# Two chunks of channels multiplied for 15 steps of the q, k, v stage while the third chunk's statistics are made, and put back into PSUM in their steps

## The chip, the cores and the metric

The kernel runs on one core of a Trainium2 chip. A core has five engines, each with its own queue of instructions that it works off in order: TensorE (PE, with its weight loads shown apart as PEld), VectorE (DVE), ScalarE (ACT), GpSimd (POOL) and SyncE (SP, which here only issues transfers). ACT and POOL issue transfers as well. Matrix products land in PSUM[...]; everything else on the chip lies in SBUF. The metric is the device time of one execution in microseconds (us), lower is better. A change of less than 0.2% can't be told from none.

## The reference

The input x is one image of 384 channels and 192 x 192 pixels in fp32. Two layers follow each other, and both add to x. Only the first one's beginning matters here:

```
g  = group_norm(x, 32 groups of 12 channels, eps 1e-5)     # no gain, no offset
qkv = w_qkv (1152 x 384) @ g + b_qkv                       # at every pixel
qkv = max over 2 x 2 pixels                                # 96 x 96 left
qkv = depthwise 3 x 3 convolution + b_dw                   # 'SAME'
q, k, v = thirds of the channels; 8 heads of 48 channels
attn = (q/|q|) (k/|k|)^T over pixels, 48 x 48 per head; four top-k softmaxes, summed; times v
x = x + repeat2x2(gelu(...)) @ w_proj + b_proj
```

The second layer is again a group norm, followed by seven depthwise convolutions (up to 13 x 13) that the kernel has folded into one, and is added to x.

The group norm needs the mean and the variance of 12 channels over all pixels before the first product can be made, so x is read once for the statistics and again for the products.

## The kernel before, in words

The 384 channels are three chunks (`NJ`) of 128 partitions. A group has 12 channels, so chunks 0 and 1 together hold 21 whole groups and 4 channels of a 22nd, whose other 8 channels are the first of chunk 2.

**Statistics stage.** The first two row blocks of x, in halves, are loaded by SP as four tiles `xt` (`load`), all three chunks at once; they stay for the next stage. The rest of each chunk comes as 22 blocks (`NX`) of 1536 pixels, chunk after chunk, in tiles `xs` of a ring of ten, loaded by ACT's queue and SP's (`load_block`, L200). VectorE takes each in three `bn_stats` of 512 columns (L236), and after a chunk's last block one `bn_aggr` (L240) gives mean and variance per channel, `mv0`. `group_stats` then goes from channels to groups and back with tiny products (with the matrices `gm` and `gmt`): mean per group (L106), broadcast (L114), variance (L123), reciprocal square root (`rsqrt`, with one ACT step), broadcast of scale and offset (L134). It is a generator, so that its pieces can be put between other work; here it runs in one go (`in_one`). The result is `gn0`, scale and offset per channel (L244).

POOL meanwhile folds the seven filters into one, `wf`; SP writes it to memory (`wfd`) at the end of the stage.

**q, k, v stage.** A loop over 48 row blocks B: for B below 24 (`NB`) q and k are made, for the 24 after that v, with x read a second time. A block is 8 rows of pixels, worked in two halves `sb`; a step is one half and one chunk m of 128 output channels, so a q, k block has 12 steps and a v block 6. In a step:

- `project` makes 2 rows x 3 input chunks j of products with 384 columns (L350) into a PSUM tile `qkv`[...]. Two such tiles take turns. The trace counts two passes for each fp32 product.
- `pool`: VectorE takes the maximum of 2 x 2 pixels (L361), after which the step after next can use the PSUM tile, and ACT adds the bias and writes it into `pooled` (L368).
- `normalize` applies `gn0` to a third of a half of the next block's x on ACT (L327), in steps 6 to 11 of a block.
- after the second half of an m: `begin` on ACT (L381), eight taps of the depthwise convolution on VectorE in the second and third step after (`taps`, L397), and `end` on ACT in the fourth: the squares with their sum (L411) and the copy of two halo rows (L416).
- after the last m of a block, in steps 3 to 6 of the next: transposes of q and k (L426), their copies on ACT (L428) and the Gram products (L438).
- in step 8 of a q, k block `strip`, an ACT copy (L457), and POOL's transfers: parts of the filter matrices. They use the memory of `v`, which is empty until block 24.

The order inside the stages is written out (`manual_schedule`): each engine takes its instructions as the program names them. What stands outside such a stretch (clearing `pooled`, L314; loading biases, L276 to L280) is put by the planner where it is ready, and where its memory is free.

After it come attention, the projection and the second layer's convolution, which the change leaves as they are but for the pool that one small tile (`gx`) comes from.

Of the kernel before, what the change touches and what calls it, by code (L numbers as in the profile page):

```python
# [7 lines left out]
F32 = mybir.dt.float32  # L8
AF = mybir.ActivationFunctionType
ALU = mybir.AluOpType  # L10
AX = mybir.AxisListType
PSUM = bass.MemoryType.PSUM
DRAM = bass.MemoryType.DRAM

P = 128
C = 384
NJ = C // P
H = W = 192
HW = H * W
HS = WS = 96  # L20
NG = 32
HEADS = 8
CH = C // HEADS
NPR = HEADS // 2
P2 = 2 * CH
KEEP = (CH // 2, CH * 2 // 3, CH * 3 // 4, CH * 4 // 5)
BRANCHES = ((5, 1), (7, 1), (5, 2), (3, 3), (3, 4), (3, 5))
K0 = 13
# [7 lines left out]
BR, BC = 8, 16  # L36
# [21 lines left out]
def tile_attn_then_large_kernel_conv(ctx: ExitStack, tc: tile.TileContext, a: dict, out: bass.AP):  # L58
    nc = tc.nc
    x = a["x"]  # L60
# [16 lines left out]
    gm = const.tile([P, NJ, NG], F32, name="gm")  # L77
    nc.sync.dma_start(out=gm, in_=a["gm"].rearrange("(j p) g -> p j g", p=P))
    gmt = const.tile([NG, C], F32, name="gmt")
    nc.sync.dma_start(out=gmt, in_=a["gmt"])  # L80
# [19 lines left out]
    def group_stats(pool, psum, mv, name, js=range(NJ)):  # L100


        own = slice(js[0], js[-1] + 1)
        ps = psum.tile([NG, 1], F32, tag="gs", name=f"{name}_ps")
        for j in js:
            nc.tensor.matmul(ps, lhsT=gm[:, j, :], rhs=mv[:, j, 0:1], start=(j == js[0]), stop=(j == js[-1]))  # L106
        mean = pool.tile([NG, 1], F32, name=f"{name}_mean")
        nc.vector.tensor_copy(mean, ps)
        yield
        yield  # L110

        pb = psum.tile([P, NJ, 1], F32, tag="gs", name=f"{name}_pb")
        for j in js:
            nc.tensor.matmul(pb[:, j], lhsT=gmt[:, j * P : (j + 1) * P], rhs=mean, start=True, stop=True)  # L114
        s = pool.tile([P, NJ, 1], F32, name=f"{name}_s")
        nc.vector.tensor_sub(s[:, own], mv[:, own, 0:1], pb[:, own])
        nc.vector.tensor_mul(s[:, own], s[:, own], s[:, own])
        nc.vector.tensor_add(s[:, own], s[:, own], mv[:, own, 1:2])
        yield
        yield  # L120
        pv = psum.tile([NG, 1], F32, tag="gs", name=f"{name}_pv")
        for j in js:
            nc.tensor.matmul(pv, lhsT=gm[:, j, :], rhs=s[:, j], start=(j == js[0]), stop=(j == js[-1]))  # L123
        var = pool.tile([NG, 1], F32, name=f"{name}_var")
        nc.vector.tensor_copy(var, pv)
        r = yield from rsqrt(pool, var, 1e-5, name)
        sb = pool.tile([NG, 2], F32, name=f"{name}_sb")
        nc.vector.tensor_copy(sb[:, 0:1], r)
        nc.vector.scalar_tensor_tensor(sb[:, 1:2], mean, -1.0, r, ALU.mult, ALU.mult)
        yield  # L130
        yield
        pc = psum.tile([P, NJ, 2], F32, tag="gs", name=f"{name}_pc")
        for j in js:
            nc.tensor.matmul(pc[:, j], lhsT=gmt[:, j * P : (j + 1) * P], rhs=sb, start=True, stop=True)  # L134
        return pc

    def in_one(gen):

        while True:
            try:  # L140
                next(gen)
            except StopIteration as e:
                return e.value


    R = 4
    NB = HS // R
# [16 lines left out]
    mv0 = const.tile([P, NJ, 2], F32, name="mv0")  # L164
    with (
        tc.tile_pool(name="s1", bufs=1) as s1,
        tc.tile_pool(name="sx", bufs=10) as sx,
# [7 lines left out]
        FX = 2 * R * 2 * W  # L175
        FB = 1536
        NX = (HW - FX) // FB
        NS0 = 2 * 2 * 2
        stats = s1.tile([P, NJ, NS0 + NX * (FB // 512), 6], F32, name="stats")
# [13 lines left out]
        xss = []  # L193

        def load_block(n):
            j, b = divmod(n, NX)
            xt = sx.tile([P, FB], F32, name=f"xs_{n}", tag="xs")

            eng = nc.scalar if n < 8 or n % 2 == 1 else nc.sync
            eng.dma_start(out=xt, in_=x[j * P : (j + 1) * P, FX + b * FB : FX + (b + 1) * FB])  # L200
            xss.append(xt)

        for n in range(2):
            load_block(n)
# [6 lines left out]
        for n in range(2, 10):  # L211
            load_block(n)
# [16 lines left out]

        for n in range(NJ * NX):  # L230
            if n in (1, 3, 5, 7):
                rows_stats(n // 2)
            j, b = divmod(n, NX)
            xt = xss.pop(0)
            for q in range(FB // 512):
                nc.vector.bn_stats(stats[:, j, NS0 + b * (FB // 512) + q, :], xt[:, q * 512 : (q + 1) * 512])  # L236
            if n + 10 < NJ * NX:
                load_block(n + 10)
            if b == NX - 1:
                nc.vector.bn_aggr(mv0[:, j, :], stats[:, j].rearrange("p n s -> p (n s)"))  # L240
        nc.sync.dma_start(
            out=wfd.rearrange("(j p) s -> p j s", p=P), in_=wf.rearrange("p j x y -> p j (x y)")
        )
        nc.vector.tensor_copy(gn0, in_one(group_stats(s1, s_ps, mv0, "g0")))  # L244
# [7 lines left out]
    with ExitStack() as ctx_v:  # L252
        vpool = ctx_v.enter_context(tc.tile_pool(name="vpool", bufs=1))
        NM = 3 * NJ
        NEG = -(2.0**127)
        v = vpool.tile([P, NJ, HS, WS], F32, name="v")
        ssq = vpool.tile([P, 2 * NJ, NB], F32, name="ssq")
        bd = vpool.tile([P, NPR, P], F32, name="bd")
        ctx_a, ctx_qk = ExitStack(), ExitStack()
        gps = ctx_a.enter_context(tc.tile_pool(name="gram", bufs=1, space=PSUM))  # L260
        gram = gps.tile([2 * CH, NPR, 2 * CH], F32, name="gram")
        a2 = ctx_a.enter_context(tc.tile_pool(name="a2", bufs=1))
        aw = ctx_a.enter_context(tc.tile_pool(name="aw", bufs=1))
        qkvps = ctx_a.enter_context(tc.tile_pool(name="qkvps", bufs=2, space=PSUM))
# [4 lines left out]
        wqk = a1.tile([P, NJ, 2 * C], F32, name="wqk")  # L269
        wv = a2.tile([P, NJ, C], F32, name="wv")  # L270
        wqkv = a["wqkvT"].rearrange("(j p) o -> p j o", p=P)
# [20 lines left out]

        free = v.rearrange("p j h w -> p (j h w)")
        ZQ = 32 * NJ // NB
# [30 lines left out]
        def normalize(B, sb, j):  # L325
            xt = xts[B, sb]
            nc.scalar.activation(xt[:, j], xt[:, j], AF.Identity, bias=gn0[:, j, 1:2], scale=gn0[:, j, 0:1])  # L327
# [14 lines left out]

        def project(B, m, sb):

            ps = qkvps.tile([P, SR, 512], F32, tag="qkv", name="qkv")
            xt = xts[B, sb]
            wq, mm = (wqk, m) if m < 2 * NJ else (wv, m - 2 * NJ)
            for r in range(SR):
                for j in range(NJ):
                    nc.tensor.matmul(  # L350
                        ps[:, r, : 2 * W],
                        lhsT=wq[:, j, mm * P : (mm + 1) * P],
                        rhs=xt[:, j, r * 2 * W : (r + 1) * 2 * W],
                        start=(j == 0),
                        stop=(j == NJ - 1),
                    )
            return ps
# [284 lines left out]
        def begin_attention():  # L642
# [4 lines left out]

        steps = [
            (B, u, (2 * NJ if B >= NB else 0) + u // 2, u % 2)
# [3 lines left out]
        with tc.manual_schedule():  # L653
            nc.sync.dma_start(out=wqk, in_=wqkv[:, :, : 2 * C])
# [4 lines left out]
            for s, (B, u, m, sb) in enumerate(steps):  # L659
# [8 lines left out]
                pool(m, sb, project(B, m, sb))  # L668
# [46 lines left out]
        with (  # L715
            tc.tile_pool(name="bx", bufs=3) as bx,
            tc.tile_pool(name="b1", bufs=1) as b1,
# [28 lines left out]
            with tc.manual_schedule():  # L746
# [13 lines left out]
                for b in range(NBB):  # L760
# [19 lines left out]
                    g = b1.tile([P2, NBK], F32, tag="gx", name=f"gx_{b}", bufs=3)  # L780
# [441 lines left out]
```

## Time and profile before

| what | us |
|---|---|
| median of three runs | 3096.77 (3096.74 to 3097.59) |
| the profiled execution | 3095.74 |
| its span | 3094.0 |
| statistics stage, to the last `bn_aggr` | 0 to 154.1 |
| group statistics | 154.1 to 160.7 |
| a block of q and k (12 steps), TensorE's time | 50.46 |
| TensorE busy over the span | 2913.6 (94%) |
| VectorE busy | 2529.4 (82%) |
| ACT busy | 1247.2 (40%) |
| POOL busy | 915.6 (30%) |

A row of the chain names what the end of the program was waiting for at that time, so time taken out elsewhere is worth nothing until the chain moves there. A row of the groups gives line, engine, operation, tile written and read, shapes and count, then busy time, mean length in ns, and the engine's idle time before it with what ended it. Lengths of neighbouring instructions overlap a little: 66 `bn_stats` of 676 ns each took 39.12 us, 593 ns from start to start. Such spacings, not lengths, add up to time.

### The profile page before, as it was taken

The numbers are of one execution on the slowest core, as the hardware profiler recorded it, in microseconds if no ns is written. First come the engines' busy times: TensorE is split into PE (matmuls) and PEld (weight loads), VectorE is DVE, ScalarE is ACT, GpSimd is POOL, SyncE is SP. The second block draws the span as 40 slices with busy tenths as digits, with TensorE's granted clock in tenths as the row PEclk, the third lists the DMA queues.
The fourth block names the chain that finished last, engine by engine and source line by source line (L and its number), as shares of the span: only waits on it lengthen the run. The fifth ranks groups of instructions, "written<-read, shape, count | busy, mean of one in ns | idle before, by whom it ended". The sixth has DMA issues, their size and how long they took to land.

```text
span 3094.0 us, 31922 instructions
## 1 busy us (share of the span) xinstructions
PE 2913.6 (94%) x10794; PEld 1938.3 (63%) x10794; DVE 2529.4 (82%) x3459; ACT 1247.2 (40%) x2339; POOL 915.6 (30%) x1103
## 2 busy tenths in 40 slices
PE   0099999999999999999999999999999999999998
PEld 0056666666666666666555555555777777777776
DVE  8968887878787878788999899878778777777775
ACT  0034444444444444444444444733333333333332
POOL 3033232424232323222223222500433333333331
PEclk9999999999999999999999999999999999999999
DMA  9933433334342424233333332577999999999994
GB/s 386 383 113 96 136 107 121 124 108 143 89 153 77 155 80 152 87 122 104 125 104 101 103 128 71 168 217 198 263 263 247 241 247 246 246 248 244 244 218 116
DMA packets 276307, 523.95 MB, mean 169 GB/s; under 512 B 26866, under 2 KB 190768, under 8 KB 276144
## 3 DMA queue, kind: packets, MB, share of 16 engines
q1 hardware_dynamic: 204880, 327.00, 39.6%
q0 software_dynamic: 45040, 151.32, 16.2%
q10 hardware_dynamic: 26224, 43.59, 3.8%
q8 instruction: 86, 1.41, 0.2%
q14 instruction: 77, 0.63, 0.1%
HBM read 360.46 MB, written 161.37 MB: 169 GB/s over the span
## 4 chain that ended last, share of the span: by engine, by line
PE 87%; DVE 10%; DMA 1%; issue 1%; ACT 0%; POOL 0%; SPq 0%; ACTq 0%; DVEq 0%; POOLq 0%
PE qkv L350 49%; PE conv L1012 29%; PE pj L1074 3%; DVE stats L236 3%; DVE v L397 3%; PE av L770 2%; PE gram L438 2%; PE tr L426 2%; DVE mx L361 1%; DMA xs<-in_x 1%; DMA xt<-in_x 1%; DVE xp L994 0%; DVE cell L1090 0%; DVE stats_t L1091 0%; DVE mv L240 0%
## 5 line engine op out<-in xcount | busy, mean ns | idle before, releaser
L350 PE MATMUL qkv<-xt,wqk 128*128 128x384 f32 x3456 | 1132.6, 487 | 1.3 <-ACT xt L327 1.3
L350 PEld LDWEIGHTS qkv<-xt,wqk 128*128 128x128 f32 x3456 | 650.3, 190 | 435.7 <-ACT xt L327 2.1
L1012 PE MATMUL conv<-xp,wt 128*128 128x288 f32 (+1 forms) x3840 | 917.7, 402 | 2.5 <-ACT co L1020 2.5
L1012 PEld LDWEIGHTS conv<-xp,wt 128*128 128x128 f32 x3840 | 729.0, 190 | 188.8 <-ACT co L1020 2.9
L397 DVE SCALAR_TENSOR_TENSOR acc<-pooled,wd,acc 128x384 f32<-128x384 f32 (+2 forms) x1152 | 732.8, 636 | 30.6
L361 DVE TENSOR_REDUCE mx<-qkv 128x192 f32<-128x768 f32 x432 | 412.6, 955 | 241.0 <-PE qkv L350 229.3
L368 ACT ACTIVATE pooled<-mx,bq 128x192 f32<-128x192 f32 x432 | 196.8, 456 | 962.1 <-DVE mx L361 961.8
L994 DVE STREAM_TRANSPOSE xp<-xn 128x4608 f32<-128x4608 f32 (+1 forms) x107 | 442.1, 4132 | 173.2 <-PE conv L1012 165.7
L350 PE MATMUL qkv<-xt,wv 128*128 128x384 f32 x1728 | 563.8, 487 | 1.7 <-ACT xt L327 1.1
L350 PEld LDWEIGHTS qkv<-xt,wv 128*128 128x128 f32 x1728 | 325.6, 190 | 234.4 <-ACT xt L327 7.5
L1020 ACT ACTIVATE co<-conv,cb 128x288 f32<-128x288 f32 x384 | 191.1, 499 | 598.0 <-PE conv L1012 587.8
L335 POOL TENSOR_TENSOR sum<-xt 128x192 f32<-128x192 f32 x144 | 97.2, 675 | 1109.8 <-ACT xt L327 1097.5
L397 DVE SCALAR_TENSOR_TENSOR v<-pooled,wd,v 128x384 f32<-128x384 f32 (+2 forms) x576 | 376.6, 654 | 15.2
L327 ACT ACTIVATE xt<-xt,gn 128x768 f32<-128x768 f32 x288 | 285.2, 1014 | 2.9 <-DVE gn L244 2.9
L1037 POOL DMA_DIRECT2D out<-o x191 | 105.8, 584 | 567.3 <-DVE o L1028 519.2
L971 POOL TENSOR_TENSOR raw<-raw,up 128x2496 f32<-128x2496 f32 x46 | 230.8, 5016 | 26.8 <-DMA up<-pd 26.8
L1028 DVE STREAM_TRANSPOSE o<-co 128x2304 f32<-128x2304 f32 (+1 forms) x50 | 209.9, 4201 | 19.8 <-ACT co L1020 19.8
L106 PE MATMUL g_ps<-mv,gm 128*32 128x1 f32 x18 | 1.8, 186 | 156.3 <-DVE mv L240 153.6
L1074 PE MATMUL pj<-v,wp 128*128 128x384 f32 x432 | 144.2, 493 | 0.6 <-ACT gx L781 0.6
L236 DVE BATCH_NORM_STATS2 stats<-xs 128x6 f32<-128x512 f32 x198 | 118.2, 676 | 1.8 <-DMA xs<-in_x 1.7
L1074 PEld LDWEIGHTS pj<-v,wp 128*128 128x128 f32 x432 | 81.9, 192 | 56.0 <-ACT gx L781 1.2
L336 POOL TENSOR_TENSOR sum<-sum,xt 128x192 f32<-128x192 f32 x144 | 113.2, 786 | 11.3
(171 smaller groups left out, 1730.7 us busy)
## 6 DMA issues: line engine op xcount, KB each, us to landing
xt<-in_x SPq DMA_DIRECT2D x96, 1152.0 KB, 7.2
wt<-zd SPq DMA_DIRECT2D x46, 1536.0 KB, 13.1
raw<-in_x SPq DMA_DIRECT2D x182, 312.0 KB, 13.1
out<-o POOLq DMA_DIRECT2D x188, 288.0 KB, 6.8
zd<-v POOLq DMA_DIRECT2D x96, 416.0 KB, 4.6
up<-pd SPq DMA_DIRECT2D x184, 156.0 KB, 12.2
xs<-in_x ACTq DMA_DIRECT2D x37, 768.0 KB, 13.1
xs<-in_x SPq DMA_DIRECT2D x29, 768.0 KB, 15.0
```

Of the source, the lines that this page charges most:

```text
L236: nc.vector.bn_stats(stats[:, j, NS0 + b * (FB // 512) + q, :], xt[:, q * 512 : (q + 1) * 512])
L327: nc.scalar.activation(xt[:, j], xt[:, j], AF.Identity, bias=gn0[:, j, 1:2], scale=gn0[:, j, 0:1])
L350: nc.tensor.matmul(ps[:, r, : 2 * W], lhsT=wq[:, j, mm * P : (mm + 1) * P], rhs=xt[:, j, r * 2 * W : (r + 1) * 2 * W], start=(j == 0), sto ...
L361: nc.vector.tensor_reduce(mx, ps[:, :, : 2 * W].rearrange("p r (y w x) -> p r w y x", y=2, x=2), AX.XY, ALU.max,)
L368: nc.scalar.activation(pool_t[m][:, k : k + SR, 1 : 1 + WS], mx, AF.Identity, bias=bq[:, m : m + 1])
L397: nc.vector.scalar_tensor_tensor(acc[:, :nt], pool_t[m][:, k0 + dy : k0 + dy + nt, dx : dx + WS], wd[:, m, t : t + 1], acc[:, :nt], ALU.mu ...
L971: eng.tensor_add(rv, rv, uv.unsqueeze(2).to_broadcast([P, (m1 - m0) * WS, 2]))
L994: nc.vector.transpose(bass.AP(at.tensor, at.offset, [list(at.ap[0]), [NBQ, n], [1, NBQ], [NQ * NBQ, CC], [ME * NBQ, NE]],), bass.AP(row.te ...
L1012: nc.tensor.matmul(ps[:, t0:t1], lhsT=wt[:, c, o : o + P], rhs=d[:, c, g + 2 * t0 : g + 2 * t1 - 1 : 2, :], start=(g == 1), stop=(g == NGR ...
L1020: nc.scalar.activation(co[:, c], ps, AF.Identity, bias=cb[:, cc : cc + 1])
L1028: nc.vector.transpose(bass.AP(at.tensor, at.offset, [list(at.ap[0]), [2 * W, n], [BC, NBQ], [W, 2], [1, BC]]), bass.AP(of.tensor, of.offse ...
L1074: nc.tensor.matmul(ps, lhsT=wp[:, j, i * P : (i + 1) * P], rhs=v[:, j, b * RB : (b + 1) * RB, :].rearrange("p r w -> p (r w)"), start=(j = ...
```

## The change

After chunk 1's statistics are done, and while those of chunk 2 are made, scale and offset of chunks 0 and 1 are worked out (the group that reaches into chunk 2 gets its eight missing channels from a transfer of their own, `spare`, with statistics `sy`). With them TensorE multiplies chunks 0 and 1 for the first half (`sb` 0) of row blocks 0 to 4 and the three q chunks: 15 steps, list `EARLY`. Each result is copied by ACT from PSUM to `begun`. In the step itself ACT copies it back into a PSUM tile (`fill`, one step ahead), and `project` only adds the products of chunk 2.

What this takes along:

- `v`, `wqk` and the PSUM tiles of the q, k, v stage are set up before the statistics stage. The x blocks that the early products read stay (`kept`, in the memory of `v`); so do the results. Of the ring of ten, five tiles lie in `v` as well.
- `group_stats` can have a further column (`NJ`, the eight channels), and with `apart` it yields between a product and its reader. `early` is advanced once after each `bn_stats` of chunk 2; after its small operations it names all its products in one piece. The final group statistics use chunks 1 and 2 only.
- of `wqk`, the q columns of chunks 0 and 1 are loaded late in chunk 0; the rest after the last x block. Odd blocks of chunk 2 are loaded by POOL's queue in place of ACT's.
- the steps of a q, k block go q0, k0, q1, k1, q2, k2 in place of q0, q1, q2, k0, k1, k2.

```diff
-    gm = const.tile([P, NJ, NG], F32, name="gm")
+    GY = 2 * P // (C // NG)
+    NY = (GY + 1) * (C // NG) - 2 * P
+    gm = const.tile([P, NJ + 1, NG], F32, name="gm")
...
+    gmt = const.tile([NG, C + P], F32, name="gmt")
+    nc.sync.dma_start(out=gmt[:, :C], in_=a["gmt"])
+    nc.gpsimd.memset(gm[:, NJ], 0.0)
+    nc.gpsimd.memset(gm[:, NJ, GY : GY + 1], NY / P / (C // NG))
+    nc.gpsimd.tensor_copy(gmt[:, C:], gmt[:, 2 * P - 1 : 2 * P].to_broadcast([NG, P]))
...
+    NKEEP = 2
+    EARLY = [(B, m) for B in range(5) for m in range(NJ)]
...
+        def load_blocks():
+            while waiting:
+                n = waiting[0]
+                j, b = divmod(n, NX)
+                if (j, b) in kept:
+                    xs = kept[j, b]
+                elif ring:
+                    xs = ring.pop(0)
+                else:
+                    return
+                other = nc.scalar if j < 2 else nc.gpsimd
+                eng = other if n < 8 or n % 2 == 1 else nc.sync
+                eng.dma_start(out=xs, in_=x[j * P : (j + 1) * P, FX + b * FB : FX + (b + 1) * FB])
...
+        def early():
+            pc = yield from group_stats(s1, s_ps, mv0, "ge", (0, 1, NJ), True)
+            yield
+            nc.vector.tensor_copy(gn0[:, :2], pc[:, :2])
...
+            ready(0)
+            for n, (B, m) in enumerate(EARLY):
+                if m == 0:
+                    ready(B + 1)
+                ps = qkvps.tile([P, SR, 512], F32, tag="qkv", name="qkv")
+                for r in range(SR):
+                    for j in range(2):
+                        nc.tensor.matmul(
+                            ps[:, r, : 2 * W],
+                            lhsT=wqk[:, j, m * P : (m + 1) * P],
+                            rhs=half[B][j][:, r * 2 * W : (r + 1) * 2 * W],
+                            start=(j == 0),
+                            stop=(j == 1),
+                        )
+                nc.scalar.copy(halved(begun[B, m]), ps[:, :, : 2 * W])
...
                 nc.vector.bn_stats(stats[:, j, NS0 + b * (FB // 512) + q, :], xt[:, q * 512 : (q + 1) * 512])
-            if n + 10 < NJ * NX:
-                load_block(n + 10)
+                if j == 2:
+                    next(first, None)
+            if (j, b) not in kept:
+                ring.append(xt)
+            for _ in load_blocks():
+                pass
+            if n == NX - 4:
+                for jj in range(2):
+                    nc.sync.dma_start(out=wqk[:, jj, :C], in_=wqkv[:, jj, :C])
+                y0 = 2 * P
+                nc.sync.dma_start(
+                    out=spare, in_=x[y0 : y0 + NY, :].rearrange("c (k n) -> (c k) n", k=P // NY)
+                )
+            if n == NX + 10:
+                w = HW * NY // P // 6
+                sy = s1.tile([P, 6, 6], F32, name="sy")
+                for q in range(6):
+                    nc.vector.bn_stats(sy[:, q, :], spare[:, q * w : (q + 1) * w])
+                nc.vector.bn_aggr(mv0[:, NJ, :], sy.rearrange("p n s -> p (n s)"))
...
+        nc.sync.dma_start(out=wqk[:, 2, :C], in_=wqkv[:, 2, :C])
+        nc.sync.dma_start(out=wqk[:, :, C:], in_=wqkv[:, :, C : 2 * C])
...
-        nc.vector.tensor_copy(gn0, in_one(group_stats(s1, s_ps, mv0, "g0")))
+        pc = in_one(group_stats(s1, s_ps, mv0[:, :NJ], "g0", (1, 2)))
+        nc.vector.tensor_copy(gn0[:, 2:], pc[:, 2:])
...
         def normalize(B, sb, j):
+            if B < NKEEP and sb == 0 and j < 2:
+                return
...
+        def fill(B, m, sb):
+            if sb == 0 and (B, m) in begun:
+                ps = qkvps.tile([P, SR, 512], F32, tag="qkv", name="qkv")
+                nc.scalar.copy(ps[:, :, : 2 * W], halved(begun[B, m]))
+                filled.append(ps)
+
         def project(B, m, sb):
-            ps = qkvps.tile([P, SR, 512], F32, tag="qkv", name="qkv")
+            js = range(NJ)
+            if filled:
+                ps, js = filled.pop(), (NJ - 1,)
+            else:
+                ps = qkvps.tile([P, SR, 512], F32, tag="qkv", name="qkv")
...
+        turns = [m + s * NJ for m in range(NJ) for s in range(2)] + [2 * NJ + m for m in range(NJ)]
...
-            nc.sync.dma_start(out=wqk, in_=wqkv[:, :, : 2 * C])
+            fill(0, 0, 0)
...
-                pool(m, sb, project(B, m, sb))
+                ps = project(B, m, sb)
+                if s + 1 < len(steps):
+                    n = steps[s + 1]
+                    fill(n[0], n[2], n[3])
+                pool(m, sb, ps)
...
+            tc.tile_pool(name="bg", bufs=3) as bg,
...
-                    g = b1.tile([P2, NBK], F32, tag="gx", name=f"gx_{b}", bufs=3)
+                    g = bg.tile([P2, NBK], F32, tag="gx", name=f"gx_{b}")
```

## The prediction

> **What bounds the kernel now.** I read the chain that ended last first, then the table of stretches, then single rows. The chain, in order of time (start, length, engine and line, count):
>
> ```profile
> 22.97 0.37 SPq L654
> ...
> 23.99 23.82 DMA xs<-in_x
> ...
> 112.78 39.12 DVE stats L236 x66
> ...
> 160.54 0.18 DVE gn L244
> 160.74 1.04 ACT xt L327
> 161.82 60.13 PE qkv L350 x180
> ...
> 222.60 3.87 PE qkv L350 x12
> 226.48 0.68 PE gram L438 x8
> 227.15 0.65 PE tr L426 x6
> ```
>
> Up to 47.8 us the chain runs through transfers, to 154.1 through VectorE's statistics without a gap, then through 6.6 us of small dependent steps (154.10 to 160.72), and from 161.8 through TensorE alone. The stretches (length, then busy time and count of PE, PEld, DVE, ACT, POOL, then granted clock, DMA share, GB/s):
>
> ```profile
> 112.80:154.10 41.30, 0.27 (x2) 0.18 (x2) 41.25 (x67) 0.00 (x0) 0.00 (x0) 1.00 0.88 358
> 154.10:161.80 7.70, 3.59 (x20) 3.28 (x20) 2.02 (x14) 1.26 (x3) 0.19 (x1) 1.00 0.00 1
> 322.90:373.30 50.40, 50.40 (x188) 31.20 (x186) 40.95 (x60) 23.18 (x49) 15.65 (x21) 1.00 0.38 121
> ```
>
> TensorE is idle while chunk 2's statistics are made, but VectorE has nothing to spare there. A q, k block of 12 steps takes 50.46 us and TensorE fills it; VectorE has 41.0 us of work in it. So a TensorE microsecond removed from a block is worth one only until VectorE's 41 us are near.
>
> **What is removed.** One pass of 384 columns takes 3.87 / 12 = 0.323 us (an fp32 product is two passes), a step of 12 passes 3.87 us. Fifteen steps lose 2 rows x 2 chunks x 2 passes: 120 passes, **38.7 us**. A filled step keeps 4 passes, 1.29 us.
>
> **When the early work can start.** Chunk 1's statistics end at 112.78. Ahead of that:
> - The weight transfer (1.18 MB) no longer goes out on SP's queue at 22.97, ahead of the blocks that the chain waits for; VectorE's one wait on xs, 1.7 us at 42.3, goes: -1.7.
> - Eight channels more: six BATCH_NORM_STATS2 of 384 columns, at 0.46 us between 0.593 for 512 (39.12 / 66) and 0.33 for 256 (the pitch of that form), 2.8 us, and an aggregate over 36 values, 0.2 us by length from 2.16 for 444 (L240): +3.0.
> - Transfers: 0.39 MB of weights and 1.18 MB of the eight channels, 3.8 us at the 418 GB/s of this stretch, for the 2.8 us taken out. SP issues them in front of later xs blocks. VectorE is only some 2 us behind the transfers (the last byte lands near 148.5, the last block is begun at 150.1), so I add 1.0, between 0 and 3.
>
> Chunk 2 begins at 115.1. The twelfth statistic of it has the 14 small operations of the first group statistics interleaved: 12 x 0.593 + 14 x 0.18 (their spacing in the 154 to 159 chain) = 9.6. The yields put one to three statistics (0.6 to 1.8 us) between each small matmul and its reader; the longest, the six-pass broadcast, took 1.45, so I charge no wait; without that cover it is 1 to 2 us. First scale and shift at 124.7, first normalised tile 1.04 later, TensorE starts at 125.8. ACT's ten normalisations (1.01) and fifteen copies from PSUM (0.8 to 1.0) are 24 us beside 39 us of TensorE, hidden.
>
> **How long it lasts.** [...] The row first (TensorE's weight loads in order of time; start, length):
>
> ```profile
> 164.54 0.34 PEld L350 LDWEIGHTS qkv<-xt,wqk 128*128 128x128 f32 x1 [0.30 <-issue]
> 165.18 0.34 PEld L350 LDWEIGHTS qkv<-xt,wqk 128*128 128x128 f32 x1 [0.30 <-issue]
> 165.67 0.51 PEld L350 LDWEIGHTS qkv<-xt,wqk 128*128 128x128 f32 x2
> ```
>
> Passes start 0.64 us apart here and 0.32 from 165.67 on (two loads of 0.19 in 0.51), though the granted clock reads 1.00: 3.85 us of half speed, 1.9 us lost, after an idle stretch. [...] Before, there is one start; after, two, at 125.8 and again behind the small chain, which has only tiny matmuls. By the row the second costs 1.9[...]; I take the row, and 0 as the other end[...]. So the early work is 38.7 + 1.9 = 40.6 us and ends at **166.4**. VectorE finishes chunk 2 at 115.1 + 39.1 + 2.2 + 2.5 = 158.9. The last group statistics stand behind the early products in TensorE's order, so 7.5 us stick out. This is the step that costs most: chunk 2 is not long enough to hide fifteen steps.
>
> **The chain after it.** 6.6 us before; with two chunks for three the two broadcasts have four passes for six (-0.5 each), the variance -0.2, the mean pays its third and fourth pass at the end (+0.3): 5.7. Scale and shift of chunk 2 come at 172.1, against 160.72: **+11.4**. Inside that time other costs lie hidden: the stage's tiles for q, k, v now share addresses with those of the statistics (ten 6 KB buffers before, five beside v after), so nine memsets of 0.59 us, which ran at 9 to 17 us, and three small loads on ACT's queue wait for the statistics' end; from 159 to 172 there is room, without it up to 5 us. The rest of the weights goes out on SP after the last xs and before the filter table, and has 17 us. On POOL, eleven xs issues (0.76 us each by its filter loads) fall where POOL is idle (27 to 160). The broadcast copy of gmt stands on POOL too: behind the bn load it only delays filters that nobody reads until 137; ahead of it, it delays VectorE's start by some 7 us, of which the transfer waits before 47.8 (6.1 us) swallow most. I take 0, the other end is +3.
>
> **The first step** no longer waits for three normalisations in turn (two are done): -0.5.
>
> **The filled steps.** The refill is an ACT copy into PSUM, which no row shows; the nearest are ACT's squares, which write PSUM:
>
> ```profile
> L411 ACT ACTIVATE junk<-acc 128x384 f32<-128x384 f32 x132 | 63.3, 479 | 0.0
> L411 ACT ACTIVATE junk<-acc 128x480 f32<-128x480 f32 x6 | 3.3, 558 | 0.0
> L411 ACT ACTIVATE junk<-acc 128x288 f32<-128x288 f32 x6 | 2.4, 397 | 0.2 <-issue 0.2
> ```
>
> 0.84 ns a column gives 0.80 us for 768; the normalisation (SBUF to SBUF, 768) took 1.01, my upper end. It waits for the maximum two steps back (its PSUM buffer), and on ACT for what is queued before it: the pooled write 0.36, a normalisation 0.92 where one is due, square and halo copy 0.75 (pitches). Two rates set what happens next:
>
> ```profile
> L397 DVE SCALAR_TENSOR_TENSOR acc<-pooled,wd,acc 128x384 f32<-128x384 f32 x48 | 30.6, 637 | 1.3
> L361 DVE TENSOR_REDUCE mx<-qkv 128x192 f32<-128x768 f32 x12 | 11.5, 957 | 8.2 <-PE qkv L350 8.2
> ```
>
> A step needs 0.87 (maximum) + 2.57 (four taps) = 3.44 us of VectorE. Four steps, one of them filled, are 1.29 + 3 x 3.87 = 12.9 us on TensorE and 13.8 on VectorE; the transposes and Gram products (4.0 us a block) let VectorE catch up in steps 3 to 6. Followed from the end of step 7: maxima end 0.97 + 3.44 each, step 10's at 11.3, TensorE is through step 11 at 12.9, and the next block's first refill is there at 11.3 + 0.36 + 0.92 + 0.75 + 0.8 = 14.1. TensorE waits 1.2, and 2.0 with the taps stretched to 2.7 to 3.0 us where POOL adds (as in the trace at 456 to 463). Block 0 has three-row taps (2.17), so it hands on only 0.4 to 1.1. Refills at steps 4 and 8 are within 0.3 of being in time. Sum: 0.7 + 3 x 1.7 + some 1.2 = **+7**, between 1 (VectorE never late) and 15 (VectorE and TensorE add up at each refill).
>
> The order of m (q and k in turn) keeps the last pair last, so the Gram products come as before. After block 4, and in the later stages, I find nothing to cost; moved gelu buffers there are 0, within 2 either way.
>
> **Sum.** -38.7 + 11.4 - 0.5 + 7 = -20.8. Against the profiled execution: span 3094.0 becomes 3073.2, its time 3095.74 (1.7 around the span) 3074.9; the median of the runs, 3096.77, is 1.0 above that execution: **3076**.
>
> **Rivals.**
> - No stalls[...] (0.14): -38.7 + 9.5 - 0.5 + 1 to 3: about 3069. For it: VectorE's 41.0 is under the 42.7 that TensorE keeps per block. Against: the four-step count.
> - VectorE becomes the bound in blocks 0 to 4 (0.14): stalls of 15 or more, 3085 to 3091. For it: 41 of 42.7, and SCALAR_TENSOR_TENSOR stretched by POOL.
> - Chunk 2's odd blocks, through POOL's queue, arrive late (0.05): it costs one for one only if the first four blocks are late or VectorE ends past 166, over 7 us late; then 3080 to 3090.
> - The early work does not stick out (0.03): 3066. It would have to start before 118, when chunk 1 has only just ended.
> - Slower (0.04): each refill holds its step. Net of the +11.4, the change has 27.8 us to lose, or 1.85 us per filled step; I count 0.5. If writing PSUM[...] made a refill 3 to 4 us, 15 x 3 = 45 us of waiting gives about 3114. Against: ACT's squares write PSUM beside TensorE now, at 0.48.
>
> The main case (0.60) runs from 3072 to 3083. Eight in ten needs parts of the first two rivals: 3067 to 3089. What can be told from no change is 0.2%, 6.2 us. Faster 0.92: all of the main case and the cheaper rivals; same 0.04 from the tail of VectorE's; slower 0.04.
>
> **What would show it.** Early products from about 126 to 166 with the first passes at 0.64; the last group statistics' first matmul held by TensorE's own queue, not by VectorE; scale and shift near 172; blocks 1 to 4 at 43.5 to 45.5 us with TensorE waiting on an ACT copy at their first step; block 5 at 50.46. Wrong if chunk 2 starts after 120, if a refill takes over 1.5 us, or if stalls pass 15.

## The result and the profile after

| | before | after |
|---|---|---|
| median of the runs (us) | 3097.16 (4 runs, 3096.74 to 3097.59) | 3081.45 (4 runs, 3081.00 to 3082.22) |
| ratio | 1 | 0.995 (0.9932 to 0.9967) |
| span of the profiled execution (us) | 3094.0 | 3079.0 |

The changed kernel is faster by 15.7 us in the medians and 15.0 us in the two profiled spans. The forecast was 3076 and -20.8: the direction and most of the mechanism held, and some 5 us of the gain are missing.

The chain of work that ended last, of the kernel after (start, length, engine and line, count), around the early products:

```profile
91.65 2.77 DVE sy L358 x6
126.76 40.97 PE qkv L324 x120
168.19 0.61 PE g_pb L125 x4
171.60 0.81 PE g_pc L149 x4
172.55 0.34 ACTq L391
172.93 0.47 ACTq L392
173.44 0.55 ACTq L395
174.05 1.03 ACT xt L441
175.12 37.01 PE qkv L478 x108
```

Before, this stretch was VectorE's alone up to 154; now 41 us of it are TensorE's (L324), and the small group statistics stand at the end of those. Three instructions of ACT's queue, L391 to L395, are new in the chain: three small loads issued between the last statistic and the first normalisation.

VectorE's timeline shows who is late for whom at the end of chunk 2 (the bracket is the idle time before the row and its releaser), and where it waits for data earlier:

```profile
89.77 1.88 DVE L340 BATCH_NORM_STATS2 stats<-xs 128x6 f32<-128x512 f32 x3 [4.51 <-DMA xs<-in_x]
...
167.99 0.15 DVE L119 COPY g_mean<-g_ps 32x1 f32<-32x1 f32 x1 [8.18 <-PE g_ps L115]
```

VectorE had nothing to do for 8.18 us before it could copy the mean: the product that makes the mean was queued on TensorE behind the early steps. The first row is a wait of 4.51 us in chunk 1. SP issued the added transfers from 68.88 to 73 us, ahead of it, while the transfers ran at 416 GB/s without a gap; that these cost the wait is argued, since no run leaves them out.

The stretches of the kernel after (length; busy time and count of PE, PEld, DVE, ACT, POOL; granted clock; DMA share; GB/s), first the restart of the q, k, v stage, then block 2 to 3, from first transposes to first transposes:

```profile
172.00:174.00 2.00, 0.39 (x2) 0.30 (x2) 0.16 (x1) 0.00 (x0) 1.41 (x3) 0.50 0.10 22
...
176.00:178.00 2.00, 2.00 (x5) 1.09 (x4) 0.00 (x0) 1.83 (x2) 1.92 (x5) 0.50 0.21 28
178.00:180.00 2.00, 2.00 (x7) 1.17 (x6) 0.96 (x1) 0.46 (x1) 1.62 (x3) 0.84 0.19 28
...
270.38:315.99 45.61, 43.59 (x164) 26.38 (x163) 40.95 (x61) 25.21 (x52) 15.47 (x21) 1.00 0.39 130
```

A block lasts 45.61 us where it lasted 50.4; TensorE is busy for 43.59 of it, where it was busy throughout. VectorE has the same 40.95 us. TensorE's waits from 175 to 480 us (total, times, longest), on the refill, on the first normalisation and, for the last of six transposes, on VectorE's taps:

```profile
PE qkv L478 <- ACT qkv L464: 4.2, 3, 1.4
PE qkv L478 <- ACT xt L441: 2.7, 1, 2.7
PE tr L555 <- DVE acc L526: 1.6, 3, 0.5
```

L464 is the refill. Its rows show what it costs, and what it waits for. First the group (busy time, mean ns), then the timeline of all engines at one refill of a block's first step:

```profile
L464 ACT COPY qkv<-v 128x768 f32<-128x768 f32 x15 | 12.0, 797 | 0.0
```

```profile
302.90 0.94 DVE L490 TENSOR_REDUCE mx<-qkv 128x192 f32<-128x768 f32 x1
303.77 3.33 DVE L526 SCALAR_TENSOR_TENSOR acc<-pooled,wd,acc 128x384 f32<-128x384 f32 x4
303.88 0.46 ACT L497 ACTIVATE pooled<-mx,bq 128x192 f32<-128x192 f32 x1 [1.60 <-DVE mx L490]
304.25 1.01 ACT L441 ACTIVATE xt<-xt,gn 128x768 f32<-128x768 f32 x1
305.16 0.47 ACT L540 ACTIVATE junk<-acc 128x384 f32<-128x384 f32 x1
305.91 0.79 ACT L464 COPY qkv<-v 128x768 f32<-128x768 f32 x1
306.75 9.39 PE L478 MATMUL qkv<-xt,wqk 128*128 128x384 f32 x28 [1.39 <-ACT qkv L464]
```

The refill takes 0.80 us. It is late because the maximum ended at 303.84 and ACT, which had waited 1.60 us for that maximum, then did its pooled write, a normalisation, the squares and the halo copy ahead of the refill. TensorE waits 1.39 us at the end of that row of dependent work. VectorE's four taps, from 303.77, take 3.33 us, so the next maximum begins only at 307.03, and VectorE stays behind.

A wait in these lists is shorter than what TensorE loses, because the profile gives a product 0.49 us, and this modelled end overlaps the next start. The starts of the single passes give the whole loss, against a pitch of 0.3226 us. From 175 to 480 us:

| where | us |
|---|---|
| refill at the first step of block 1 | 0.35 |
| refill at the first step of blocks 2, 3, 4 | 3 x 1.65 |
| refills at the later filled steps | 1.9 |
| last of six transposes, waiting for VectorE's taps, 3 times | 3 x 0.69 |
| sum | 9.3 |

Counted the other way: the stage has 120 x 0.323 = 38.7 us less of passes. From its first product to the seventh block's first transposes it took 363.1 us before (161.82 to 524.96) and takes 333.9 after (175.12 to 508.97), 29.3 less; so 9.4 us are lost.

### The profile page after: what moved, and what is told of

It reads as the page before. It is cut to its first block, busy times and chain, and to the rows that moved or that the text cites. A ratio compares the mean times of both kernels' runs of the same rounds, so it can differ in the third digit from the quotient of the medians.

```text
span 3079.0 us, 32033 instructions
## 1 busy us (share of the span) xinstructions
PE 2921.3 (95%) x10812; PEld 1940.1 (63%) x10812; DVE 2534.9 (82%) x3481; ACT 1272.8 (41%) x2376; POOL 921.9 (30%) x1117
## 4 chain that ended last, share of the span: by engine, by line
PE 85%; DVE 10%; DMA 3%; issue 1%; ACT 1%; POOL 0%; ACTq 0%; SPq 0%; DVEq 0%; POOLq 0%
PE qkv L478 46%; PE conv L1148 29%; DVE v L526 3%; PE pj L1210 3%; PE av L906 2%; DVE mx L490 2%; PE gram L567 2%; DVE acc L526 2%; PE tr L555 2%; PE qkv L324 1%; DMA v<-in_x 1%; DVE stats L340 1%; DMA xs<-in_x 1%; DMA xt<-in_x 1%; DVE xp L1130 0%
## 5 line engine op out<-in xcount | busy, mean ns | idle before, releaser
L478 PE MATMUL qkv<-xt,wqk 128*128 128x384 f32 x3336 | 1096.4, 487 | 7.4 <-ACT qkv L464 4.2
L478 PEld LDWEIGHTS qkv<-xt,wqk 128*128 128x128 f32 x3336 | 626.4, 190 | 429.6 <-ACT qkv L464 10.1
L1115 ACT ACTIVATE xn<-raw,par 128x2112 f32<-128x2112 f32 x48 | 102.8, 2142 | 1.2 <-ACT pjs L1218 1.2
```

The lines of the kernel that those rows point to most:

```text
L478: nc.tensor.matmul(ps[:, r, : 2 * W], lhsT=wq[:, j, mm * P : (mm + 1) * P], rhs=xt[:, j, r * 2 * W : (r + 1) * 2 * W], start=(j == 0), sto ...
```

## The experiments

The statistics stage differs from run to run (the first scale and shift stands between 124.7 and 128.9 us in profiles of the same code for that stage), so a difference of less than a microsecond in a median is taken as shown only if a profile shows the mechanism. The changed kernel was measured twice, with medians of 3081.45 and 3081.95 and nine executions between 3080.85 and 3083.95. Most variants differ from it by less than the 0.2% named at the start; such a difference is taken as one where the executions lie wholly outside that range and a profile shows where the time went.

### Three early steps fewer

```diff
-    EARLY = [(B, m) for B in range(5) for m in range(NJ)]
+    EARLY = [(B, m) for B in range(4) for m in range(NJ)]
```

> Only the 12 early steps of row blocks 0 to 3 are kept; block 4's three are made in full in their steps. Early products then end 7.75 us sooner, at about 160.0, where VectorE ends too (159.8). Theory A (what sticks out past the statistics only changes its place, and each block with filled steps pays its own waits, 2.9 us): the 7.75 us come back in block 4, its waits go; 2.9 us faster than the changed kernel, about 3078.5, block 4 at 50.5 us. Rival (what sticks out is lost as such, since the group statistics wait for it): 7.75 us faster, about 3073.7. Rival (the waits belong to the whole stretch and not to the block): within 1 us of 3081.45.

Measured: 3078.16 us (3077.11 to 3078.84), 0.9939 (0.9925 to 0.9954) of the kernel before: 3.3 us faster than the changed kernel. The early products end at 159.3 and the stage begins at 166.77, 8.35 earlier:

```profile
159.30 0.29 PE L115 MATMUL g_ps<-mv,gm 128*32 128x1 f32 x4
166.77 3.57 PE L478 MATMUL qkv<-xt,wqk 128*128 128x384 f32 x5 [2.96 <-ACT xt L441]
```

Blocks 1 to 4 last 45.19, 45.49, 46.27 and 50.47 us. The last three steps only changed their place: they took 7.75 us off the stage, cost as much in front of it, since VectorE was through with chunk 2 at 159.2 here (159.8 in the changed kernel), and brought a block with late refills besides. Fifteen steps are too many for this cover.

### The three small loads ahead of the wait

The biases and filters of q and k move to the pool that lives through both stages, and are loaded in the statistics stage:

```diff
+    bq = aq.tile([P, NM], F32, name="bq")
+    wd = aq.tile([P, NM, 9], F32, name="wd")
+    bdw = aq.tile([P, NM], F32, name="bdw")
...
             if n == NX - 4:
+                nc.scalar.dma_start(out=bq[:, :nqk], in_=a["b_qkv"][:, :nqk])
...
-        bq = a2.tile([P, NM], F32, name="bq")
...
-        nc.scalar.dma_start(out=bq[:, :nqk], in_=a["b_qkv"][:, :nqk])
```

> The three small loads (bq, wd, bdw) that ACT issues between scale and shift (172.43) and the first normalisation (174.05) get memory of their own and are issued in the middle of chunk 0. Theory: ACT's issuing is what holds the normalisation; TensorE begins the stage 1.4 us sooner, 3080.0. Rival (the profile's own attribution: the normalisation waited for POOL's memsets of pooled, which also begin at 172.6): no change, 3081.4, the normalisation still near 174.

Measured: 3080.60 us (3078.98 to 3082.54), 0.9948 (0.9933 to 0.9963). The median moved 0.85 us, less than its scatter. The timeline shows the mechanism:

```profile
174.27 4.82 POOL L425 MEMSET pooled<- 128x588 f32 x9 [31.88 <-DVE gn L378]
174.30 3.78 ACT L440 ACTIVATE xt<-xt,gn 128x768 f32<-128x768 f32 x4 [2.40 <-DVE gn L378]
```

The first normalisation begins 0.2 us after the copy of scale and shift (174.1 here, the statistics being 1.7 us later in this execution), where the changed kernel had 1.6, and the first product 1.28 after it instead of 2.7. POOL's memsets still run from 174.27 to 179.1, and the normalisation starts beside the first of them. In the changed kernel's profile the normalisation's idle time was put down to those memsets; this run refutes that. The loads were the cause, and they waited because the memory of their tiles came free only when the last statistic was copied.

### The last statistics between the early steps

```diff
-        pc = in_one(group_stats(s1, s_ps, mv0[:, :NJ], "g0", (1, 2)))
+        chain = group_stats(s1, s_ps, mv0[:, :NJ], "g0", (1, 2))
+        for pieces in (2, 2, 1):
+            for _ in range(pieces):
+                next(chain)
+            f, key = held.pop(0)
+            f(*key)
+        pc = in_one(chain)
```

`held` has the last three early steps, `f` computes one.

> The small products of the last group statistics are put between early steps 12 and 13, 13 and 14, 14 and 15 instead of behind all of them; nothing else changes. Theory: the chain of 5 us runs beside the last two or three early steps, scale and shift of chunk 2 come near 168.5 instead of 172.4: 4 us faster, 3077.5, and if the shorter pause leaves the array's clock up (no passes of 0.64 us after it) nearly 2 more, 3075.5. Rival (each small product now waits behind a whole early step of 2.58 us, so the chain only stretches): 3080 to 3082.

Measured: 3077.43 us (3074.90 to 3079.66), 0.9935 (0.9918 to 0.9951). TensorE's timeline: the last small product of the chain, then the first product of the stage.

```profile
170.03 0.60 PE L149 MATMUL g_pc<-g_sb,gmt 32*128 32x2 f32 x4
173.37 9.05 PE L489 MATMUL qkv<-xt,wqk 128*128 128x384 f32 x22 [2.73 <-ACT xt L452]
```

Scale and shift came at 170.7, not at the 168.5 expected: every small product stands behind a whole early step, with some 0.5 us of its own. The stage began 1.75 us earlier than in the changed kernel, less than half of the 4.9 us chain. The passes after it still started 0.64 us apart, and 22 of them took 9.05 us where the pitch of 0.3226 makes 7.3: here half speed followed a pause of 2.73 us behind full products, without the rest of the chain. The median is 4.0 us lower, as expected, but the profile accounts for 1.75 of it; it is of the slowest of the four executions, and what the others had more is not shown. So the expected number came out with half of its mechanism, and that is luck.

### Less work for VectorE in the filled blocks

The last tap of each half of the filter is left out for q and k in blocks 0 to 4, so this kernel computes less:

```diff
-            for t in ((0, 1, 2, 3), (5, 6, 7, 8))[half]:
+            for t in ((0, 1, 2, 3), (5, 6, 7, 8))[half][: 3 if b < 5 and m < 2 * NJ else 4]:
```

> Left out: the last tap of each half (two of the eight on VectorE) for q and k in blocks 0 to 4, so those blocks' q and k are not the reference's; VectorE has some 7.5 us less per block. Theory (VectorE is late in filled blocks): blocks 1 to 4 fall from 45.2 to 46.4 us to about 43, some 8 us faster in all, near 3073.5. Rival (the refill's own place on ACT's queue, behind normalisation, squares and halo copy): the wait of 1.4 us at each block's first step stays, 1 to 3 us faster, 3078.5 to 3080.5.

Measured: 3075.48 us (3075.07 to 3076.64), 0.9932 (0.9917 to 0.9946), 6.0 us less than the changed kernel where 8 were expected. The stretch of the same block, and the wait on the refill that is left in the list of TensorE's waits:

```profile
269.71:313.18 43.47, 43.27 (x163) 26.56 (x162) 33.22 (x48) 25.21 (x52) 15.09 (x21) 1.00 0.41 136
```

```profile
PE qkv L478 <- ACT qkv L464: 0.4, 1, 0.4
```

With VectorE at 33.2 us a block is 43.47 us long, and the transposes wait no more. The 0.75 us above 42.72 (50.47 less 24 passes) are two refills that come 0.37 late each by the starts of the passes. VectorE's work is therefore the cause of about 6 of the 9.3 us. That the rest comes from ACT's order, the refill standing behind ACT's other work, is argued here; the next runs move the refill.

### The refill ahead of ACT's other work

```diff
+                taken = take()
+                if s + 1 < len(steps):
+                    n = steps[s + 1]
+                    fill(n[0], n[2], n[3])
                 for f, args in late.pop(s, ()):
                     f(*args)
...
-                ps = project(B, m, sb)
-                if s + 1 < len(steps):
-                    n = steps[s + 1]
-                    fill(n[0], n[2], n[3])
+                ps = project(B, m, sb, taken)
```

> The refill of the next step is put on ACT's queue ahead of what else the step leaves there (begin, squares, halo copy, copies of transposes), no other change. Theory (VectorE is behind in a filled block; the refill's place only adds to it): the refill that comes 1.4 us late at a block's first step comes some 0.7 us sooner, but VectorE's work stays; 1.5 to 2.5 us faster than the changed kernel, about 3079.5. Rival (ACT's queue is the cause): the waits of 1.4 us go and blocks fall to 43.5; 6 us faster, about 3075.5. Rival (VectorE alone decides): no change, 3081.4.

Measured: 3100.58 us (3097.63 to 3103.00), 1.0012 (1.0005 to 1.0019): 19 us slower than the changed kernel, and 3.9 us above the kernel before, which is less than the 0.2% that can be told. A wait in TensorE's list that was not there:

```profile
PE qkv L479 <- DVE mx L491: 18.8, 14, 2.8
```

The edit did more than it was meant to. PSUM tiles of one name were handed out here in the order in which they are first written; with the refill written first, it took the tile that comes free earlier, and the unfilled step ahead of it was left with the tile whose maximum had only just begun. Fourteen steps waited for it. So this run says nothing on ACT's order, and it shows by accident how the change could have lost: the same 15 refills, with their tiles the other way round, give back the whole gain.

To put ACT's order alone to the test, the tiles were named by the parity of their step as well, so that each step keeps its tile:

```diff
-                ps = qkvps.tile([P, SR, 512], F32, tag="qkv", name="qkv")
+                ps = qkvps.tile([P, SR, 512], F32, tag=f"qkv{s % 2}", name="qkv")
```

> The refill again ahead of the step's other ACT work, but each step keeps its PSUM tile by name (even steps one, odd steps the other), so that the refill can't take the tile of the step before it. Theory (VectorE is behind; the refill's place adds to it): 1.5 to 2.5 us faster than the changed kernel, about 3079.5, and TensorE's waits on the maximum of 18.8 us in the run without named tiles are gone. Rival (the extra 19 us of that run came from ACT's order, since squares and copies come later): about 3100 again. Rival (VectorE alone decides): 3081.4.

Measured: 3081.48 us (3079.10 to 3082.75), 0.9950 (0.9936 to 0.9964). The 19 us are gone, and nothing is gained:

```profile
PE qkv L479 <- ACT qkv L464: 2.9, 3, 1.0
PE qkv L479 <- DVE mx L491: 1.4, 3, 0.5
```

The refill's wait fell from 4.2 to 2.9 and another of 1.4, on the maximum, came in: 4.3 in all. The block is still 45.6 us. The refills that came 0.37 late at the later filled steps are in time here, so ACT's order did cause these; but what they no longer cost comes back at the maxima. A shorter path from maximum to refill doesn't help when the maxima themselves are late.

### POOL's sums out of the filled blocks

POOL adds up four of the six normalised tiles of each block in this stage. This kernel moves the sums of blocks 0 to 5 to the v stage:

```diff
-            if (sb * NJ + j < 4) != (B < NB):
+            if (sb * NJ + j < 4 and B % NB > 5) != (B < NB):
```

> POOL's sums of x for row blocks 0 to 5 are all made in the v stage instead of two thirds of them in the q, k stage. The four taps that take 2.7 to 3.3 us beside POOL's sums should take 2.57 in blocks 0 to 5. Theory (POOL's additions stretch the taps and this is part of the waits): 1.0 to 1.5 us a block, 4 to 5 us faster, about 3077, if v blocks 0 to 5 have room for six sums on POOL. Rival (stretched taps are hidden behind TensorE, or the v blocks pay for it): 3080 to 3083.

Measured: 3085.14 us (3082.26 to 3087.08), 0.9963 (0.9950 to 0.9976), 3.7 above the changed kernel's median, with executions that overlap with it. In its blocks the edit did what was expected: 44.14 us instead of 45.6, refill waits halved, and VectorE's busy time in the block lower by 1.6 us though it does the same work (the longest tap took 620 ns, 905 with POOL adding beside it):

```profile
273.18:317.32 44.14, 43.34 (x163) 26.52 (x162) 39.34 (x61) 25.20 (x52) 4.68 (x5) 1.00 0.37 124
```

It lost more later: from block 5's transposes to the first product with av, 1527.5 us went by where the changed kernel needed 1520.0. That is the rival, that the v blocks pay for it. TensorE's waits from 1350 to 1900 us, in the v stage, rose from 1.1 us to 4.6: on normalisations from 1.1 to 2.1, on maxima from none to 1.3, and 1.0 for which the profile names nothing. That is 3.5 of the 7.5; the rest is not accounted for. In this execution the statistics were also 3.4 us late.

### Two filled steps a block, six blocks

Twelve early steps as in the first experiment, but spread: two in each of six blocks, so that seven full steps stand between the second filled step of a block and the first of the next.

```diff
-    EARLY = [(B, m) for B in range(5) for m in range(NJ)]
+    EARLY = [(B, m) for B in range(6) for m in range(2)]
```

> Twelve early steps again, but as two of the three q chunks in six row blocks instead of three in four. Early products end near 160 as with twelve steps before. A filled block then keeps 45.3 us of TensorE's work beside some 43 of VectorE's. Theory (a block loses time because three filled steps outrun VectorE): waits of 6.6 us fall to 1 or 2, about 5 us faster than the twelve in four blocks (3078.2): 3073. Rival (every refill costs its own wait of about 0.55 us, wherever it is): 3078, as before.

Measured: 3073.64 us (3073.29 to 3075.55), 0.9929 (0.9914 to 0.9944): 7.8 us faster than the changed kernel and 4.5 faster than twelve steps with three a block. The stretch of a block:

```profile
266.65:312.87 46.22, 45.80 (x171) 28.11 (x170) 40.58 (x61) 24.60 (x51) 15.64 (x21) 1.00 0.40 127
```

A block of two filled steps lasts 46.22 us where three made 45.6: the third filled step of a block was worth 0.6 us there instead of its 2.58. Two steps take 16 passes, 5.2 us, out of 50.47, and 0.9 of this is lost again; with three it was 2.9. No refill wait is left in TensorE's list, though by the starts of the passes one refill in a block comes 0.37 late. The transposes wait for VectorE's taps:

```profile
PE tr L555 <- DVE acc L526: 1.3, 4, 0.3
```

### Together

The two edits that are independent, two steps a block and the earlier loads:

> Twelve early steps as two chunks in six blocks, and the three small loads issued in chunk 0 with memory of their own. Theory: both gains add, since the one lies before the stage and the other in its blocks: 1.4 us below the kernel without the second edit, about 3071.6. Rival (the loads delay chunk 0's statistics by as much as they free later): no gain over it, 3073.

Measured: 3072.23 us (3071.48 to 3074.04), 0.9922 (0.9906 to 0.9939). The median is 1.4 us below that of two steps a block alone, as expected. The executions of the two overlap, but the wait for the first normalisation, 2.7 us without the second edit, is shorter by as much:

```profile
PE qkv L477 <- ACT xt L440: 1.3, 1, 1.3
```

With the named PSUM tiles and the refill first as a third edit:

> Two q chunks in six blocks, the three small loads in chunk 0, and the refill ahead of the step's other ACT work with named PSUM tiles. Theory: with two filled steps a block the refills are in time anyway, so the third edit adds nothing: 3071.5 to 3072.5. Rival (refills still hold steps by a few tenths): 3070.

Measured: 3072.38 us (3071.99 to 3072.94), 0.9922 (0.9910 to 0.9935). The third edit adds nothing, and its profile shows why. By the starts of the passes no refill is late any more, but the transposes wait longer for VectorE's taps, and the block lasts 46.23 us, as before:

```profile
PE tr L555 <- DVE acc L526: 2.1, 4, 0.5
```

So VectorE sets the pace of such a block, and ACT's order only where TensorE waits for it. On the same chip the changed kernel was run again:

> The changed kernel as it is, on the same chip as the two beside it: 3081 to 3082, some 9 to 10 us above the kernel with two q chunks in six blocks; if statistics take as long as in the slowest runs so far, up to 3084.

Measured: 3081.95 us (3080.85 to 3083.95), 0.9954 (0.9941 to 0.9966). So there is a version 9.6 us faster than the changed kernel and 24.3 faster than the one before, with three early steps fewer.

## Why the forecast was right, and where it was 5 us off

The account by the two profiled executions, each term against the forecast's own:

| step of the forecast | forecast (us) | measured (us) |
|---|---|---|
| passes removed | -38.7 | -38.7 (120 passes at 0.323) |
| scale and shift of chunk 2 later | +11.4 | +11.9 |
| small loads on ACT's queue "hidden" | 0 | +1.4 |
| first step no longer waits | -0.5 | 0 |
| waits at filled steps | +7 | +9.4 |
| later stages | 0 | -0.4 and +1.4 |
| sum | -20.8 | -15.0 |

**The start of chunk 2** came at 116.5, not 115.1. The wait of 1.7 us at 42.3 went and the statistics of the eight channels took 2.77 us, both as forecast. The 1.0 charged to the added transfers was too little if the wait of 4.5 us ahead of 89.77 is theirs. That chunk 2 came no more than 1.4 later than forecast is luck: chunk 0 was done 4.0 us earlier (67.5 for 71.5), where the forecast had 1.7.

**The early products** ran from 126.76 for 40.97 us (forecast 125.8 and 40.6), and stuck out by 7.9 us behind VectorE (7.5). The chain behind them took 4.9 us (5.7). These small errors nearly cancel, which is luck: +11.9 for +11.4. What the forecast called the costliest step was sized well, and the first experiment confirmed that the last steps of the fifteen earn nothing. (Its cheap rival, early work that does not stick out, is 3068.5 by the forecast's own terms, not 3066; the case did not arise.)

**The second start at half speed** is there. The passes from 175.12 start 0.64 us apart until 178.5 and the granted clock stands at 0.50, 0.50 and 0.84 in the stretches from 174 to 180, which is 1.7 us lost where the forecast took 1.9. The rival in which it costs nothing, +9.5 in place of +11.4, is refuted. That half speed would come again behind the small chain was the author's estimate from the one start in the trace before. The clock of 1.00 that the forecast read beside the same spacing before was a misreading: the trace of the kernel before has no record of the clock ahead of 165.50, and a stretch without a record reads 1.00.

**"Hidden between 159 and 172"** failed for the small loads. The forecast saw that they wait for the statistics' memory and took VectorE's end (159.8) as the time at which it comes free. It came free at the last copy of the statistics, 172.6, when nothing covers them. The forecast's 5 us for the uncovered case was an upper end; 1.4 is what it was, since POOL's memsets, equally late, held up nobody.

**The first step's -0.5** was not to be had: with its refill late by 0.35 and one by 0.16 the first 50 us save 9.9 of 10.3, and nothing beyond the passes is gained. The first passes start 0.80 and then 0.64 us apart in both profiles: at half speed TensorE was no faster than the three normalisations of 1.01 us each, so there was no wait to take away.

**The waits at the filled steps** were followed correctly and summed too short. The forecast's 0.7 at block 1 was 0.35, its 3 x 1.7 at blocks 2 to 4 was 3 x 1.65, its "some 1.2" for the later refills 1.9. What the sum left out is that VectorE, late after three filled steps, also holds up the next consumer of its work, the transposes: 3 x 0.69. The forecast had let VectorE "catch up in steps 3 to 6" without asking who reads its results there. Leaving out taps and moving POOL's sums shortened the blocks, and spreading the filled steps cut what a block loses from 2.9 to 0.9 us; a shorter path through ACT did neither. So the rate of VectorE decides, short of the rival "VectorE becomes the bound" with 15 us of stalls.

**The refill** took 0.80 us, as the rows of ACT's squares gave it. The slower rival, 3 to 4 us for a refill, is refuted; but with the PSUM tiles in the wrong order the time was that of the kernel before or longer, with fourteen steps waiting for a maximum.

**POOL's queue** and the broadcast copy of gmt cost nothing: VectorE waited for no block of chunk 2, and the batch normalisation's first VectorE row moved from 8.00 to 8.16 us.

**The later stages** were taken as 0. They differ by one stretch at a granted clock of 0.50 in each kernel, at different places. The kernel before has its own in the projection, after TensorE had waited 1.83 us for statistics; the changed kernel has none there:

```profile
2111.10:2114.50 3.40, 3.40 (x7) 1.89 (x6) 3.12 (x7) 0.58 (x1) 0.00 (x0) 0.50 1.06 272
```

These 1.7 us (the 12 passes after the wait took 5.83 us, 4.14 in the changed kernel) are mostly given back, since TensorE then waits less for VectorE (the changed kernel has a wait of 1.05 at the last group product that the one before has not). So up to the first convolution product the time won rose only by 0.4 to 16.4; then 1.4 were lost in the convolution, at one place. The stretches there, after and before:

```profile
2154.00:2156.00 2.00, 2.00 (x7) 1.50 (x8) 0.74 (x2) 1.04 (x3) 0.76 (x1) 0.74 1.06 343
2156.00:2158.00 2.00, 2.00 (x6) 1.47 (x5) 0.96 (x1) 0.00 (x0) 2.00 (x1) 0.50 1.06 372
```

```profile
2172.00:2174.00 2.00, 2.00 (x10) 1.61 (x9) 0.10 (x1) 0.50 (x1) 1.85 (x1) 1.00 1.07 373
```

Each kernel has one pause of TensorE at the end of the first 40 passes of the convolution. Before, it was 2.48 us and the clock stayed at 1.00; after, it was 2.20 us and the clock fell to 0.74 and 0.50, so that 110 passes took 28.19 us, 1.7 more than the 26.50 that they took in the last version.

## What to carry to other kernels

Work that is pulled forward into another engine's time is worth its own time only while that cover lasts and only as fast as its consumer can take the shorter steps: count the consumer's rate per group of steps, and follow its lateness to everything that reads its results, not only to the next refill. Then take the smaller amount, and spread it: here twelve steps, two in a block, gave 23 us where fifteen, three in a block, gave 15.7. At the seam of two stages, list what is issued after the last instruction that frees the first stage's memory; loads in that list can be on the path even when they are small, as three were here for 1.4 us.

## What the runs showed of the hardware that was not expected

**The length of a pause does not tell whether half speed follows.** Twelve profiles of the changed kernel and its variants have the same pause in the convolution, 2.20 to 2.21 us. In eleven of them 1.7 us were lost afterwards: in nine, 110 passes took 28.19 us, and in the runs with the sums moved and with the refill first, 92 took 23.91 and 70 took 18.64. In one, the last version, they were not lost: 110 passes took 26.50 us, 0.24 each. Its stretch, at the same place:

```profile
2146.00:2148.00 2.00, 1.47 (x6) 1.23 (x7) 1.28 (x5) 1.66 (x4) 0.00 (x0) 1.00 1.03 252
2148.00:2150.00 2.00, 2.00 (x10) 1.57 (x10) 0.17 (x1) 0.50 (x1) 1.80 (x1) 1.00 1.07 377
```

The kernel before had the longer pause there, 2.48 us, and lost nothing: 60 passes took 14.58 us, 0.24 each, as well. In the projection it is the other way round. After waits of the same length for statistics, 1.83 us in the kernel before and 1.84 in the changed one, the former ran at a granted clock of 0.50 from 2111.1 to 2114.5, and the latter at 1.00. What decides is not shown, since no run varied a pause on purpose.

So whether the 1.4 us lost in the convolution belong to the change is not shown either. The start of the stage varies too: after a wait of 1.31 us in both, the first 44 passes took 17.23 us in the version with two edits, and the first 156 took 52.19 in the last version. The pitch of 0.3226 makes 14.4 and 50.5, so 2.9 and 1.7 us were lost.

**VectorE's taps are slower while POOL adds**: four taps took 3.33 us in the row at 303.77 where they take 2.57 in others, and a block's VectorE time fell from 40.95 to 39.34 us when POOL's sums were taken out of it.
